# Causal attention on one core: the softmax's probabilities are turned block by block on VectorE and carried to their keys by transfers within SBUF, in place of transposes on TensorE

## The chip, the core and the metric

The kernel runs on one core of one Trainium2 chip. The time is the device time of one execution in microseconds (us). The core has TensorE (PE; its weight loads are listed apart as PEld), VectorE (DVE), ScalarE (ACT), GpSimd (POOL) and SyncE (SP), which here only issues transfers. Each engine works through its own list of instructions strictly in order. Transfers (DMAs) run on the 16 DMA engines that the profile counts.

## The reference, cut to what matters

The program is one decoder layer over x of shape (4, 512, 512): a gated delta-rule attention, a cross attention with quantized operands, then a block of causal grouped-query attention and a mixture of experts. The change is in the third part:

```python
q = rmsnorm(h @ wq, qnorm_w); k = rmsnorm(h @ wk, knorm_w); v = h @ wv   # 16 heads of 128, 4 key heads
q, k = rope(q), rope(k)
scores = einsum('bhqd,bhkd->bhqk', q, k) / sqrt(128)
scores = where(causal, scores, finfo.min)
attn = softmax(scores)
o = einsum('bhqk,bhkd->bhqd', attn, v)
x1 = x + o.reshape(B, S, H * DH) @ wo
```

For `o`, the sum runs over keys. TensorE sums over the partition axis, so the probabilities, which the softmax leaves with queries on partitions, have to be turned so that keys lie on partitions.

## The kernel before, in words

The tokens are 16 tiles of 128 (`i`, four tiles to a sequence; `c = i % 4`). A tile attends to the `c + 1` tiles of its sequence up to itself, so a row of probabilities has `nk = 128 * (c + 1)` entries. The 16 query heads are taken as 4 groups `g` of 4 heads `n` that share one key head.

- `scores(i, g)`, lines 1316 to 1345: for each head one f32 matmul of 128 queries by `nk` keys (L1333), the causal mask (L1335), the row maximum (L1336, L1337), the exponential on ACT (L1339), and the division by the row sum on DVE (L1341, L1343). The result is four tiles `e[n]` of queries x keys; even groups use the buffers `xa`, odd ones `og` and `x_in`, one set each.
- `values(g, e)`, lines 1354 to 1373: for each key tile `k`, four TensorE transposes (L1364), a copy of the four results from PSUM to SBUF on ACT (`eT`, L1366, three buffers), and one f32 matmul of 512 columns that adds to `po` (L1370, and L1360 for the last `k`). Then DVE copies `po` to `oT` (L1372).
- `project(g)`, lines 1375 to 1382: four f32 matmuls of 512 columns per group, `oT` times the output weights (L1380), with the weights' next pieces loaded by SP into three buffers (`wot`, `c_o`; `load_o`, L1239).
- `attention(i)` runs `scores(g + 1)`, `project(g - 1)`, `values(g)` for each g; the first group of the next tile is scored under the last group of this one.

Around it, `weave` (L155) mixes five streams into one program: attention of tile i, q/k/v projections of a later tile (`qkv`, weights through four `c_q` buffers, L1230 and L1267), the cross attention of a later tile (`crossing`, L283 to L371), the end of an earlier tile (`rest_of`, L1421) and the routing of tokens to experts. Each stream is a generator; `weave` advances the stream with the lowest due time, and `steps` (L152, L153) says how many pauses a stream is expected to have, so how much of a tile's time one pause stands for. ACT, DVE and POOL keep the order of this program; PE's and SP's lists are ordered by the scheduler that builds the program. At the end `load_experts` (L1690 to L1694) loads 12 MB of expert weights through SP while the last tiles are attended to, and the experts follow.

SP issues every one of these loads. A transfer counts into one of eight semaphores in turn, and an issue waits until the transfer eight before it has landed. So at most eight are on their way.

Of the kernel before, what the change touches and what calls it, by code (L numbers as in the profile page):

```python
# [31 lines left out]
F32 = mybir.dt.float32  # L32
BF16 = mybir.dt.bfloat16
AF = mybir.ActivationFunctionType
ALU = mybir.AluOpType
# [4 lines left out]
P = 128  # L40
B, S, D = 4, 512, 512
NT = B * S // P
TB = S // P
KD = D // P
# [60 lines left out]
def decoder(ctx: ExitStack, tc: tile.TileContext, a: dict, out: bass.AP):  # L105
    nc = tc.nc
# [6 lines left out]
    ident = tab[:, C_ID, :]  # L113
# [36 lines left out]
            yield from g  # L150

    steps = {"first_o": 3, "cross": 37, "qkv": 12, "rest_of": 5, "route": 10, "enter": 8, "spares": 24, "load": 26}  # L152
    steps.update((f"attention{c}", n) for c, n in enumerate((37, 41, 53, 57)))  # L153

    def weave(*streams):  # L155

# [53 lines left out]
    def transposed(src, pool, name, bufs=2):  # L210

        kind, eye = (F32, ident) if src.dtype == F32 else (BF16, ident_i)
        tp = p_b.tile([P, KD, P], kind, name="pb")
        for kd in range(KD):
            nc.tensor.transpose(tp[:, kd, :], src[:, kd * P : (kd + 1) * P], eye)
        t = pool.tile([P, KD, P], kind, name=name, bufs=bufs)
        nc.scalar.copy(t, tp)
        return t
# [23 lines left out]
    hTs, x2s, xis, fronts = {}, {}, {}, {}  # L242
# [135 lines left out]
    with ExitStack() as st:  # L378
# [18 lines left out]
        p_b = st.enter_context(tc.tile_pool(name="a_pb", bufs=4, space=PSUM))  # L397
# [675 lines left out]
        start = prologue(0)  # L1073
# [68 lines left out]
    with ExitStack() as st:  # L1142
        keep = st.enter_context(tc.tile_pool(name="b_keep", bufs=1, reuse_waits="tile"))
        small = st.enter_context(tc.tile_pool(name="b_small", bufs=4, reuse_waits="tile"))
        p_b = st.enter_context(tc.tile_pool(name="b_pb", bufs=6, space=PSUM, reuse_waits="tile"))
# [3 lines left out]
        wa = st.enter_context(tc.tile_pool(name="b_a", bufs=2, reuse_waits="tile"))  # L1149
        mid = st.enter_context(ExitStack())  # L1150
        wq_ = mid.enter_context(tc.tile_pool(name="b_q", bufs=2, reuse_waits="tile"))
# [39 lines left out]
        def norms(i):  # L1191


            x2 = x2s.pop(i)
            x3 = wq_.tile([P, D], F32, name="x3", bufs=1)
            yield from layernorm(x3.unsqueeze(1), x2.unsqueeze(1), small)
            nc.sync.dma_start(x3d[i], x3)
            h = wq_.tile([P, D], F32, name="h3", bufs=1)
            ss = small.tile([P, 1], F32, name="rms_s")
            nc.scalar.activation(h, x3, AF.Square, accum_out=ss)  # L1200
            yield
            r = small.tile([P, 1], F32, name="rms_r")
            rsqrt(r, ss, small, add=1e-6, mul=1.0 / D)
            yield
            nc.vector.tensor_scalar(h, x3, r, None, ALU.mult)
            yield
            tp = p_b.tile([P, KD, P], F32, name="pb")
            hTs[i] = wq_.tile([P, KD, P], F32, name="hT", bufs=2)
            for kd in range(KD):
                nc.tensor.transpose(tp[:, kd, :], h[:, kd * P : (kd + 1) * P], ident)  # L1210
            for kd in range(KD):
                nc.scalar.activation(hTs[i][:, kd, :], tp[:, kd, :], AF.Identity, scale=ln1[:, kd : kd + 1])
            yield
# [35 lines left out]
                load_o()  # L1249
                yield  # L1250

        zero = wa.tile([P, 4, P], F32, name="eT", bufs=3).rearrange("p a b -> p (a b)")
        nc.gpsimd.memset(zero, 0.0)
        nc.gpsimd.dma_start(hd[CAP : CAP + P], zero)
        nc.gpsimd.dma_start(spares[0 : 2 * NE * P].rearrange("(p n) c -> p (n c)", p=P), zero[:, 0 : 4 * NE])
# [60 lines left out]
        def scores(i, g, out):  # L1316

            c = i % TB
            at = (i - c) % RING
            runs = [(0, at, min(c + 1, RING - at))]  # L1320
            if at + c + 1 > RING:
                runs.append((RING - at, 0, at + c + 1 - RING))
            nk = (c + 1) * P
            qT, rq = qs[i]
            both = 2 if c < 2 else 1
            e = [ao.tile([P, S], F32, name="xa", bufs=4) for _ in range(4)] if g % 2 == 0 else [ao.tile([P, S], F32, name=n, bufs=2) for n in ("og", "og", "x_in", "x_in")]
            es = small.tile([P, 4], F32, name="es")
            nm = small.tile([P, 4], F32, name="nm")
            for n in range(0, 4, both):
                ps = p_b.tile([P, both, S // both], F32, name="pb")  # L1330
                for m in range(both):
                    for k, j, w in runs:
                        nc.tensor.matmul(ps[:, m, k * P : (k + w) * P], qT[g][:, n + m, :], kT[:, g, j : j + w, :], start=True, stop=True)  # L1333
                diag = ps[:, :, nk - P : nk]
                nc.vector.tensor_tensor(diag, diag, over(tab[:, C_CAUSAL, :], both), ALU.add)  # L1335
                nc.vector.tensor_reduce(nm[:, n : n + both], ps[:, :, :nk], AX.X, ALU.max, negate=True)  # L1336
                nc.vector.tensor_scalar(nm[:, n : n + both], nm[:, n : n + both], rq, None, ALU.mult)  # L1337
                for m in range(both):
                    nc.scalar.activation(e[n + m][:, :nk], ps[:, m, :nk], AF.Exp, bias=nm[:, n + m : n + m + 1], scale=rq, accum_out=es[:, n + m : n + m + 1])  # L1339
                yield  # L1340
            nc.vector.reciprocal(es, es)  # L1341
            for n in range(4):
                nc.vector.tensor_scalar(e[n][:, :nk], e[n][:, :nk], es[:, n : n + 1], None, ALU.mult)  # L1343
            out.append(e)
            yield

        def attention(i):


            c = i % TB  # L1350
            vals = [kv[k] for k in range(i - c, i + 1)]
            oTs = []

            def values(g, e):
                po = p_1.tile([P, 4, P], F32, name="po")
                eTs = []
                for k in range(c + 2):
                    if k > c:
                        yield
                        nc.tensor.matmul(po, vals[c][:, g, :], eTs[c], start=c == 0, stop=True)  # L1360
                        break
                    tp = p_b.tile([P, 4, P], F32, name="pb")
                    for n in range(4):
                        nc.tensor.transpose(tp[:, n, :], e[n][:, k * P : (k + 1) * P], ident)  # L1364
                    eT = wa.tile([P, 4, P], F32, name="eT", bufs=3)
                    nc.scalar.copy(eT, tp)  # L1366
                    eTs.append(eT)
                    yield
                    if k:
                        nc.tensor.matmul(po, vals[k - 1][:, g, :], eTs[k - 1], start=k == 1, stop=False)  # L1370
                oTs.append(wa.tile([P, 4, P], F32, name="oT"))
                nc.vector.tensor_copy(oTs[-1], po)  # L1372
                yield

            def project(g):
                oT = oTs.pop(0)
                for h in range(0, 4, 2):
                    w = ahead_o.pop(0)
                    for m in range(2):
                        nc.tensor.matmul(pw, oT[:, h + m, :], w[:, m, :], start=g == 0 and h + m == 0, stop=g == 3 and h + m == 3)  # L1380
                    load_o()
                    yield

            es = early.pop(i, [])
            if not es:
                yield from scores(i, 0, es)
            for g in range(4):
                if g < 3:
                    yield from scores(i, g + 1, es)
                elif i + 1 < NT:  # L1390
                    while i + 1 not in qs:
                        yield
                    early[i + 1] = []
                    yield from scores(i + 1, 0, early[i + 1])
                if g == 1:
                    pw = p_1.tile([P, D], F32, name="pw")
                if g > 0:
                    yield from project(g - 1)
                if g == 3:
                    x3 = wa.tile([P, D], F32, name="x3_in")  # L1400
                    nc.sync.dma_start(x3, x3d[i])
                yield from values(g, es.pop(0))
            del qs[i]
            yield
            yield from project(3)
            nc.vector.tensor_tensor(x3, pw, x3, ALU.add)
            xs[i] = x3
# [13 lines left out]
        def rest_of(i):  # L1421

            x1 = xs.pop(i)
            x2 = ao.tile([P, D], F32, name="acc", bufs=1)
            nc.sync.dma_start(x2, x2d[i])
            ss = small.tile([P, 1], F32, name="rms_s")
            h = wa.tile([P, D], F32, name="h2", bufs=1)
# [7 lines left out]
            nc.gpsimd.tensor_tensor(x2, x2, x1, ALU.add)  # L1435
            stored.append(nc.sync.dma_start(out[i * P : (i + 1) * P], x2).ins.name)
            yield
            hT = transposed(h, wa, "eT", bufs=3)
            yield

            parts = p_b.tile([P, P], F32, name="pb")
# [326 lines left out]
        def turned(b):  # L1768
            t = rows_of.pop(b)
            tp = p_b.tile([P, KD, P], F32, name="pb")  # L1770
            for kd in range(KD):
                nc.tensor.transpose(tp[:, kd, :], t[:, kd, :], ident)
            hTs[b] = wa.tile([P, KD, P], F32, name="eT", bufs=3)
            nc.vector.tensor_copy(hTs[b], tp)

        def gate_up(b):
# [128 lines left out]
```

## Time and profile before

| | |
|---|---|
| median of 3 runs | 3339.76 us (3336.23 to 3340.16) |
| profiled execution | 3333.82 us, of which the span from first to last instruction is 3332.0 us |
| mean granted TensorE clock | 0.984; 1.00 (0.99 in two stretches) in the stage that the change touches |
| the attention stage | from 1950 to 3095 us of the span |
| one tile of attention | the last add of a tile (L1406) ends at 2024.9, 2100.4, 2174.3, 2256.6, 2326.4 ... 2931.4 us: 906.5 us for 12 tiles, 75.5 us each |
| transfers that SP issues in a tile | about 30 |

"Busy" is the share of time in which an engine runs an instruction; matmuls are pipelined, so their listed durations overlap, and the cost of one is read from the distance between starts. An f32 matmul appears as two records. A group row gives count, busy time and mean duration, then the idle time of the engine just before and what ended it. The granted clock is the share of full TensorE speed.

### The profile page before, as it was taken

How to read it: one execution, taken by the hardware profiler on the slowest of the kernel's cores; microseconds unless marked ns; L12 is line 12 of the kernel's file. 1: busy time of each engine (PE TensorE's matmuls, PEld its weight loads, DVE VectorE, ACT ScalarE, POOL GpSimd, SP SyncE). 2: the span in 40 equal slices, each digit the busy share in tenths (PEclk: the TensorE clock that was granted, in tenths of full speed). 3: DMA queues.
4: the chain of work that ended last, by engine and by line, in shares of the span. 5: the costliest groups of instructions: out<-in, count | busy, mean ns of one | idle time of the engine just before them, and what ended most of it. 6: DMA issues, size and time to landing. Idle time of an engine off the chain costs nothing.

```text
span 3332.0 us, 48178 instructions
## 1 busy us (share of the span) xinstructions
PE 3170.1 (95%) x16015; PEld 1775.1 (53%) x16015; DVE 1829.9 (55%) x4184; ACT 1604.7 (48%) x4391; POOL 1460.5 (44%) x2780
## 2 busy tenths in 40 slices
PE   5899999999999999999998789999999999999998
PEld 3555555556555555555554445555555554555443
DVE  5755555546555556555454566556665666656211
ACT  3445555445554455545453345555555455644221
POOL 1156757676666766676764211112211221221442
PEclk8999999999999999999998899999999999999999
DMA  6343534444344434454434455546545555567443
GB/s 177 108 126 111 144 104 130 138 124 126 118 129 138 138 114 117 128 149 120 121 110 119 153 172 188 176 158 195 182 161 167 187 157 155 177 211 264 81 85 57
DMA packets 491033, 476.09 MB, mean 143 GB/s; under 512 B 225333, under 2 KB 340555, under 8 KB 490657
## 3 DMA queue, kind: packets, MB, share of 16 engines
q1 hardware_dynamic: 477616, 444.59, 44.3%
q0 software_dynamic: 11728, 25.58, 3.6%
q8 instruction: 128, 2.10, 0.3%
q10 hardware_dynamic: 1440, 2.84, 0.2%
q14 instruction: 121, 0.98, 0.1%
HBM read 411.23 MB, written 61.69 MB: 142 GB/s over the span
## 4 chain that ended last, share of the span: by engine, by line
PE 78%; DVE 10%; ACT 5%; issue 3%; DMA 3%; POOL 2%; SPq 0%; ACTq 0%; POOLq 0%; DVEq 0%
PE pb L598 25%; PE pb L1267 8%; PE pw L1380 5%; PE pb L972 5%; PE pb L1782 4%; DVE cv L609 3%; PE pb L1333 3%; PE po L1370 2%; PE pb L259 2%; PE pb L1364 2%; PE pb L686 2%; PE pb L671 2%; PE po L926 1%; PE po L1360 1%; PE ps L899 1%
## 5 line engine op out<-in xcount | busy, mean ns | idle before, releaser
L598 PE MATMUL pb<-xnT,w 128*128 128x512 f32 x2048 | 956.9, 602 | 0.5 <-DVE at L674 0.5
L598 PEld LDWEIGHTS pb<-xnT,w 128*128 128x128 f32 x2048 | 364.2, 192 | 337.0 <-issue 330.6
L609 DVE SCALAR_TENSOR_TENSOR cv<-pb,pp,cv 128x510 f32<-128x510 f32 (+2 forms) x576 | 424.3, 746 | 98.9 <-ACT cv L606 85.6
L752 POOL TENSOR_TENSOR iT<-iT,iW 64x126 f32<-64x126 f32 (+22 forms) x930 | 344.4, 370 | 72.9
L1267 PE MATMUL pb<-c_q,hT 128*128 128x512 f32 x768 | 352.4, 599 | 3.4 <-DMA c_q<-in_c_wq_dram 1.8
L751 POOL TENSOR_TENSOR iW<-iA,iT 64x126 f32<-64x126 f32 (+22 forms) x930 | 318.7, 343 | 65.7 <-issue 0.2
L1186 POOL TENSOR_TENSOR rope_s<-q,tab 128x128 f32<-128x128 f32 x80 | 44.9, 561 | 481.3 <-DVE q L1297 368.3
L972 PE MATMUL pb<-wot,og 128*128 128x512 f32 x512 | 246.5, 605 | 5.5 <-DVE xa L977 4.5
L1267 PEld LDWEIGHTS pb<-c_q,hT 128*128 128x128 f32 x768 | 141.4, 192 | 157.6 <-issue 146.1
L606 ACT ACTIVATE cv<-pb,pp 128x512 f32<-128x512 f32 x192 | 148.5, 774 | 146.7 <-PE pb L598 142.7
L653 POOL TENSOR_TENSOR rk<-ss,mhalf 128x8 f32<-128x8 f32 x32 | 77.9, 2436 | 277.2 <-DVE ss L652 277.2
L977 DVE TENSOR_TENSOR xa<-pb,xa 128x512 f32<-128x512 f32 x112 | 77.1, 688 | 186.9 <-PE pb L972 186.8
L306 ACT ACTIVATE x_e<-pb,nm,x_step 128x256 f32<-128x256 f32 x256 | 141.1, 565 | 58.3 <-DVE nm L302 53.6
L1333 PE MATMUL pb<-kT,qT 128*128 128x256 f32 (+3 forms) x576 | 163.2, 409 | 0.8 <-ACT og L1339 0.7
L1380 PE MATMUL pw<-wot,oT 128*128 128x512 f32 x344 | 162.5, 599 | 1.3 <-DVE oT L1372 1.3
L705 POOL TENSOR_TENSOR qg<-qh,row 128x512 f32<-128x512 f32 x64 | 83.2, 1300 | 178.5 <-ACT qh L612 155.6
L972 PEld LDWEIGHTS pb<-wot,og 128*128 128x128 f32 x512 | 92.6, 192 | 99.8 <-issue 88.0
L612 ACT ACTIVATE qh<-cv 128x512 f32<-128x512 f32 x64 | 40.4, 631 | 213.7 <-DVE cv L609 205.8
L1782 PE MATMUL pb<-w_gu,eT 128*128 x288 | 129.9, 594 | 2.8 <-issue 2.0
L1366 ACT COPY eT<-pb 128x512 f32<-128x512 f32 x160 | 91.5, 596 | 84.4 <-PE pb L1364 83.5
L458 ACT ACTIVATE em<-em,ee 128x128 f32<-128x128 f32 x256 | 78.3, 388 | 95.7 <-POOL ee L655 81.5
L1333 PEld LDWEIGHTS pb<-kT,qT 128*128 128x128 f32 x576 | 97.7, 191 | 48.6 <-issue 29.6
(436 smaller groups left out, 6171.1 us busy)
## 6 DMA issues: line engine op xcount, KB each, us to landing
c_q<-in_c_wq_dram SPq DMA_DIRECT2D x128, 512.0 KB
w<-in_a_w_dram SPq DMA_DIRECT2D x124, 512.0 KB
wot<-in_c_wo_dram SPq DMA_DIRECT2D x86, 512.0 KB
row<-g_d SPq DMA_DIRECT2D x64, 512.0 KB
c_o<-in_c_wo_dram SPq DMA_DIRECT2D x42, 512.0 KB
at_d<-at SPq DMA_DIRECT2D x64, 256.0 KB
T<-t_d SPq DMA_DIRECT2D x32, 512.0 KB
X<-x_d SPq DMA_DIRECT2D x32, 512.0 KB
```

Of the source, the lines that this page charges most:

```text
L306: nc.scalar.activation(e[:, 2 * r + g, :], ps[r][:, g, :], AF.Exp, bias=nm[:, r, g : g + 1], scale=step[:, h : h + 1], accum_out=ssum[:, g ...
L598: nc.tensor.matmul(pj, wt[:, kd, p * P : (p + 1) * P], xnT[:, kd, :], start=kd == 0, stop=kd == KD - 1)
L606: nc.scalar.activation(ac, pj, AF.Identity, bias=cb[:, m, h : h + 1], scale=cw[:, m, h, 3:4])
L609: nc.vector.scalar_tensor_tensor(ac[:, j:], pj[:, : S - j], cw[:, m, h, 3 - j : 4 - j], ac[:, j:], ALU.mult, ALU.add)
L751: eng.tensor_tensor(u, A[:, i, i + 1 :].unsqueeze(2).to_broadcast([nb, n, w]), T[:, i, :w].unsqueeze(1).to_broadcast([nb, n, w]), ALU.mult)
L752: eng.tensor_tensor(T[:, i + 1 :, :w], T[:, i + 1 :, :w], u, ALU.add)
L972: nc.tensor.matmul(pw, og[p][:, c * P : (c + 1) * P], wot[:, p, :], start=p == 0, stop=p == HG - 1)
L1267: nc.tensor.matmul(pj, hT[:, kd, :], w[:, kd % 2, :], start=kd == 0, stop=kd == KD - 1)
L1333: nc.tensor.matmul(ps[:, m, k * P : (k + w) * P], qT[g][:, n + m, :], kT[:, g, j : j + w, :], start=True, stop=True)
L1366: nc.scalar.copy(eT, tp)
L1380: nc.tensor.matmul(pw, oT[:, h + m, :], w[:, m, :], start=g == 0 and h + m == 0, stop=g == 3 and h + m == 3)
L1782: nc.tensor.matmul(pg, hT[:, kd, :], w_gu[:, bass.ds(e, 1), kd, :, :], start=kd == 0, stop=kd == KD - 1)
```

## The change

1. The transposes on TensorE and the copies to `eT` go. After the division, four VectorE instructions turn each head's probabilities in 32x32 blocks into one tile `t` (128 partitions x 4 nk, one buffer). A block transpose moves nothing out of its quarter of 32 partitions, so 16 transfers per group (four quarters q by four blocks b) bring each quarter's rows to the partitions of its keys. They are issued by SP, move 32 partitions of `nk` f32 each (16 to 64 KB), and land in the `e` tiles themselves, which now hold keys x (heads, 32 queries).
2. The value matmuls take the `e` tiles directly: 4 (c + 1) matmuls of 128 columns in place of (c + 1) of 512.
3. `po` is copied by ACT, not DVE, into its old order.
4. `steps` is set to the new numbers of pauses. Buffers are made to fit: `norms` normalizes into `x2` and `hT` and needs no `h3`; `x3_in` has one buffer, not two; `rest_of` and the experts use `hT` and `oT` where they used `eT`.

```diff
-    steps.update((f"attention{c}", n) for c, n in enumerate((37, 41, 53, 57)))
+    steps.update((f"attention{c}", n) for c, n in enumerate((79, 71, 77, 75)))
...
-            h = wq_.tile([P, D], F32, name="h3", bufs=1)
+            hTs[i] = wq_.tile([P, KD, P], F32, name="hT", bufs=2)
...
-            nc.scalar.activation(h, x3, AF.Square, accum_out=ss)
+            nc.scalar.activation(hTs[i].rearrange("p k t -> p (k t)"), x3, AF.Square, accum_out=ss)
...
-            nc.vector.tensor_scalar(h, x3, r, None, ALU.mult)
+            nc.vector.tensor_scalar(x2, x3, r, None, ALU.mult)
...
                 nc.vector.tensor_scalar(e[n][:, :nk], e[n][:, :nk], es[:, n : n + 1], None, ALU.mult)
+            yield
+
+            t = wa.tile([P, 4 * S], F32, name="eT", bufs=1)[:, : 4 * nk].rearrange("p (b k n i) -> p b k n i", b=4, n=4, i=32)
+            for n in range(4):
+                nc.vector.transpose(t[:, :, :, n, :].rearrange("p b k i -> p k b i"), e[n][:, :nk].rearrange("p (k b j) -> p k b j", b=4, j=32))
+                if n % 2:
+                    yield
+            for q in range(4):
+                for b in range(4):
+                    nc.sync.dma_start(e[q][b * 32 : (b + 1) * 32, :nk], t[q * 32 : (q + 1) * 32, b].rearrange("p k n i -> p (k n i)"))
+                yield
             out.append(e)
...
-                eTs = []
-                for k in range(c + 2):
-                    if k > c:
-                        yield
-                        nc.tensor.matmul(po, vals[c][:, g, :], eTs[c], start=c == 0, stop=True)
-                        break
-                    tp = p_b.tile([P, 4, P], F32, name="pb")
-                    for n in range(4):
-                        nc.tensor.transpose(tp[:, n, :], e[n][:, k * P : (k + 1) * P], ident)
-                    eT = wa.tile([P, 4, P], F32, name="eT", bufs=3)
-                    nc.scalar.copy(eT, tp)
-                    eTs.append(eT)
+                for q in range(4):
+                    for k, val in enumerate(vals):
+                        nc.tensor.matmul(po[:, q, :], val[:, g, :], e[q][:, k * P : (k + 1) * P], start=k == 0, stop=k == c)
                     yield
-                    if k:
-                        nc.tensor.matmul(po, vals[k - 1][:, g, :], eTs[k - 1], start=k == 1, stop=False)
                 oTs.append(wa.tile([P, 4, P], F32, name="oT"))
-                nc.vector.tensor_copy(oTs[-1], po)
+                nc.scalar.copy(oTs[-1].rearrange("p n (q i) -> p q n i", q=4), po.rearrange("p q (n i) -> p q n i", n=4))
                 yield
...
-                    x3 = wa.tile([P, D], F32, name="x3_in")
+                    x3 = wa.tile([P, D], F32, name="x3_in", bufs=1)
...
-            hT = transposed(h, wa, "eT", bufs=3)
+            hT = transposed(h, wa, "hT", bufs=1)
...
-            hTs[b] = wa.tile([P, KD, P], F32, name="eT", bufs=3)
+            hTs[b] = wa.tile([P, KD, P], F32, name=("oT", "oT", "hT")[b % 3], bufs=(2, 2, 1)[b % 3])
```

More of the change, by code (lines that the diff above doesn't have):

```diff
@@ L1204, in norms @@
             yield
-            nc.vector.tensor_scalar(h, x3, r, None, ALU.mult)
+            nc.vector.tensor_scalar(x2, x3, r, None, ALU.mult)
             yield
             tp = p_b.tile([P, KD, P], F32, name="pb")
-            hTs[i] = wq_.tile([P, KD, P], F32, name="hT", bufs=2)
             for kd in range(KD):
-                nc.tensor.transpose(tp[:, kd, :], h[:, kd * P : (kd + 1) * P], ident)
+                nc.tensor.transpose(tp[:, kd, :], x2[:, kd * P : (kd + 1) * P], ident)
             for kd in range(KD):
@@ L1250, in first_o @@
                 yield
-        zero = wa.tile([P, 4, P], F32, name="eT", bufs=3).rearrange("p a b -> p (a b)")
+        zero = wa.tile([P, 4 * S], F32, name="eT", bufs=1)[:, 0:S]
         nc.gpsimd.memset(zero, 0.0)
```

## The prediction

> **What bounds the kernel now.** I read the shares by stretch of time first, then the groups by line, then the order of time on PE, DVE and SP. By stretches (start:end, length, busy PE, PEld, DVE, ACT, POOL with counts, granted clock, DMA share, GB/s):
>
> ```profile
> 2326.00:2625.00 299.00, 294.28 (x1339) 167.61 (x1338) 187.54 (x533) 157.50 (x426) 64.87 (x92) 1.00 0.56 175
> 2625.00:2931.00 306.00, 295.99 (x1291) 157.16 (x1290) 189.84 (x546) 165.18 (x443) 68.74 (x94) 0.99 0.56 167
> 3025.00:3075.00 50.00, 49.91 (x173) 24.90 (x172) 31.78 (x97) 26.62 (x58) 5.97 (x6) 1.00 1.02 349
> 3075.00:3095.00 20.00, 20.00 (x84) 10.67 (x83) 5.98 (x21) 4.70 (x9) 5.96 (x7) 1.00 0.60 154
> ```
>
> PE is busy 97 to 100% of the attention stage, DVE 62%, ACT 53%, the DMA engines 56%; only from 3025 to 3075, while the expert weights load, are the DMA engines full too. PE's list is the bound, so PE work taken away is worth its full length as long as what feeds PE keeps up. The groups that the change removes or splits:
>
> ```profile
> L1370 PE MATMUL po<-eT,val 128*128 128x512 f32 x192 | 100.2, 607 | 1.0 <-ACT eT L1366 0.2
> L1366 ACT COPY eT<-pb 128x512 f32<-128x512 f32 x160 | 91.5, 596 | 84.4 <-PE pb L1364 83.5 <-ACT eT L1366 0.7
> L1360 PE MATMUL po<-eT,val 128*128 128x512 f32 x128 | 67.2, 607 | 0.3 <-ACT eT L1366 0.3
> L1372 DVE COPY oT<-po 128x512 f32<-128x512 f32 x64 | 43.9, 686 | 37.7 <-PE po L1360 34.7 <-issue 2.8
> ```
>
> Neither transposes nor values make PE wait long. Their true cost is the distance between starts in the order of time on PE:
>
> ```profile
> 2410.99 1.02 PE L1370 MATMUL po<-eT,val 128*128 128x512 f32 x2
> 2411.85 0.60 PE L1364 MATMUL pb<-tab,xa 128*128 128x128 f32 x4
> 2412.28 1.02 PE L1370 MATMUL po<-eT,val 128*128 128x512 f32 x2
> ```
>
> A 512-column f32 matmul (two records) takes 2411.85 - 2410.99 = 0.86 us, four transposes 0.43 us. For f32 matmuls of 128 columns with changing weights, the delta-rule stage has the row (also in order of time):
>
> ```profile
> 1000.46 0.61 PE L908 MATMUL ps<-r,X 128*128 128x128 f32 x4
> 1000.90 1.88 PE L598 MATMUL pb<-xnT,w 128*128 128x512 f32 x4
> ```
>
> Four records, two matmuls, in 0.44 us: 0.22 us each.
>
> **PE's list.** Over 16 tiles there are 4 x 40 = 160 (group, key tile) pairs. Removed: 160 x 4 transposes of 0.108 = 69 us. Values: before 160 x 0.86 = 138 us, after 640 x 0.22 = 141 us. Together **-66 us**. Separate waits come on top: in the built program the value matmuls have 503 instructions that only wait (a quarter's first matmul needs four transfers). Such an event instruction on PE's sequencer lasts 51 ns at L1364; 503 x 0.051 = 26 us if all of it shows, 0 if matmuls in flight cover it. I take half, **+13 us**, since a quarter's matmuls (0.22 to 0.88 us) are as short as two to four waits at c = 0 and longer later.
>
> **ACT and DVE.** ACT loses 160 copies (91.5 us) and gains 64 of nearly the same shape (64 x 0.596 = 38 us): no path, 0. DVE loses 43.9 us and gains 256 block transposes, 64 of each width. No row shows one. Below, the division's L1343 (0.24 us at 128, 0.48 at 512 elements); above, DVE reading PSUM (L1335 0.293 at 128, L1336 0.69 at 512); farthest, L1343's longest single record, 1.18 us. I take the PSUM row, 64 x (0.29 + 0.42 + 0.55 + 0.69) = 125 us, so DVE rises by 81 us over 1145 us, from 62 to 70%. It stays under PE; alone it costs 0, and its cover is that PE's queue is ahead of it.
>
> **SP and the transfers.** This is where I expect the price. New are 64 x 16 = 1024 issues where SP now makes about 30 per tile. The nearest rows, on SP in order of time:
>
> ```profile
> 1798.74 6.41 SPq L1103 DMA_DIRECT2D x_kT<-x_kT_d  x12
> ...
> 2431.16 0.34 SPq L271 DMA_DIRECT2D x_q_d<-x_qi  x1
> 2435.04 5.09 SPq L279 DMA_DIRECT2D x_qT<-x_q_d  x3
> ```
>
> One issue alone is 0.34 us, twelve of 32 partitions in a row 6.41 / 12 = 0.53 us. L279 must wait until L271's transfer has landed: 2435.04 - 2431.50 = 3.5 us, and 1.4 us at 1789.40, before the stage was loaded; the longest such wait is 4.6 us. I take 0.44 us an issue and 2.5 us to land: 16 x 0.44 = 7.0 us a group, 28 us a tile. The others take about 26 x 0.42 + 4 x 1.87 = 18 us a tile (L279 has four at 1.87). SP has 46 us of work in a tile of 75.5 us, so by sum it is no bound, but it works in order, and it now carries something that values wait for.
>
> The chain per group, from the last score matmul: softmax to the end of the division 6.5 us (2680.7 to 2687.2, and 2707.4 to 2714.0), block transposes 2.0 (mean of the four widths), issues 7.0, landing 2.5, so 18.0 us; plus what stands ahead in SP's queue, 0 to 8 us (the set of L279 takes 7.5), I take 4: **22 us**. Against it stands the lead: in the order in which the changed program is built, the PE work between a group's last score matmul and its first value matmul, counted with the rates above, is 22 us in the mean, but under 20 in 24 of 64 groups, under 18 in 11, and 13.6 at the least. So half of the groups would be late, by some 4 us: 32 x 4 = 128 us. A late group lets the next one's chain run on meanwhile (a group takes 75.5 / 4 = 19 us, the lead spans more than one), so I count half, **+64 us**. Bounds: at 0.34 an issue, landing 1.4 and an empty queue the chain is 15.3 us, about none late, 0; with 0.53, 4.6 us and 8 ahead it is 30 us, all 64 late by 8, half of which is 256 us.
>
> Rule against row: the Trainium skill, "DMA: Bandwidth & Descriptors", section "Bandwidth", says that transfers under 64 KB are dominated by their descriptors and should be gathered to a megabyte; these have 16 to 64 KB, which speaks against the change. Its fixed 2.0 us per transfer (section "Anatomy of one DMA", stated for GpSimd's path) would make the chain half a microsecond shorter, an estimate. No run here shows it for transfers within SBUF.
>
> **The end.** The last tiles have nothing beside them. In the built order SP issues 11 expert loads and about four other loads between the transfers of the last tile's first and second group. From 3025 to 3075 the queue moves 349 GB/s, so a 512 KB load takes 1.5 us and 15 take 22 us, where a group before took about 12 us: +10. Eight transfers in flight make the first ones after such a set land 8 x 1.5 us late, of which I count 7; the last group's chain (transposes 2.7, issues 7.0, landing 2.5 from the division's end at 3076, then 3.5 us of values) ends 3 us after the 3089.5 of now. Together **+20 us**, bounds 0 and 45.
>
> **The small edits cost 0.** `norms` writes into `x2`, which first must be stored by POOL's transfer; its six microseconds of normalization cover the 1.4 to 4.6 us that a landing takes, and 16 x 2 us off PE's path is the worst. One buffer for `x3_in`: the tile before is stored half a tile earlier. The sum of 0 stands within the other terms' width.
>
> **Sum**, in the profiled execution's own terms: 3333.8 - 66 + 13 + 64 + 20 = 3364.8. The median of the runs lies 5.9 us above that execution (3339.76 against 3333.82), so the forecast for the runs is **3371 us**, 0.9% slower. A measurement of this kernel can tell about 0.2% (7 us) from no change.
>
> **Rivals.**
> - *The lead covers the chain* (faster). For it: PE's lead grows with the pauses, 22 us in the mean; SP has 30 us free in a tile. Then lateness is 10 us, the end 10: 3333.8 - 66 + 13 + 10 + 10 = 3301, 3307 in the runs' terms. 0.33.
> - *The one tile `t` decides* (much slower, DVE and SP in turn). DVE may not turn group g + 1 before group g's 16 transfers have landed, and while DVE waits, all its other work waits. A round is transposes + issues + landing: 2.0 + 7.0 + 2.5 = 11.5 us, with L279's set inside one round of a tile some 57 us a tile, under PE's 71. With 2.7 + 8.5 + 4.6 and other loads inside (20 us) it is 83 us a tile; from 71 on it decides. 13 tiles x (83 - 75.5) = 98, with 30 at the end: 3462, 3468 in the runs' terms. 0.11.
> - *PE's list doesn't get shorter*: if 128-column passes went at the weight load's 0.190 us (LDWEIGHTS), 1280 x (0.19 - 0.11) = 102 us would eat the 66. The row at 1000.46 speaks against it. With lateness hidden by the longer list, 3333.8 - 66 + 13 + 102 + 20 = 3403, 3409. 0.04.
> - *They cancel*: lateness and end near 53 us together. 3340 give or take 7. 0.06.
>
> **How the numbers follow.** The forecast's case (3347 to 3440) has 0.46. Faster 0.33, same 0.06, slower 0.46 + 0.11 + 0.04 = 0.61. The forecast's own range is 3347 to 3440. The range for 8 in 10 reaches from 3290, below the faster case's centre, to 3455: out of it stay the lower third of the first rival (0.1) and the upper part of the second (0.07).
>
> **What would show it.** PE without transposes at L1364 and value matmuls 0.22 us apart; SP's list with 16 issues per group at 0.34 to 0.53 us; PE idle before the value matmuls put down to transfers, some 60 us in all; the tile period near 75.5 us still or above it. I am wrong if PE stays 97% busy and a tile takes 71 us (first rival), if the longest waits are DVE's transposes for transfers (second), or if value matmuls stand 0.38 us apart (third).

## The result, and the profile after

The changed kernel takes **3578.72 us** (median of 5 runs, 3575.10 to 3583.29) against 3340.16 for the kernel before (median of 5, 3336.23 to 3341.50): ratio 1.0713, 95% interval 1.0701 to 1.0725, slower by 238.6 us. The forecast was 3371 us: the sign was right, the loss over the kernel before was nearly eight times as large (238.6 us, not 31). The profiled execution took 3578.82 us.

First the engines' totals and the granted clock in 40 slices, from the page of the changed kernel:

```profile
span 3577.0 us, 51043 instructions
...
PE 3216.2 (90%) x16335; PEld 1845.4 (52%) x16335; DVE 1892.5 (53%) x4376; ACT 1555.2 (43%) x4295; POOL 1466.4 (41%) x2780
...
PEclk7999999999999999999988999989998999997999
```

Then the shares by stretch of time in the attention stage (start:end, length, busy PE, PEld, DVE, ACT, POOL with counts, granted clock, DMA share, GB/s). The first two stretches are those of the prediction:

```profile
2326.00:2625.00 299.00, 260.08 (x1225) 157.32 (x1224) 180.44 (x537) 130.50 (x361) 55.51 (x77) 0.92 0.59 177
2625.00:2931.00 306.00, 245.95 (x1068) 140.95 (x1067) 159.74 (x468) 116.64 (x329) 54.19 (x75) 0.89 0.55 166
3200.00:3330.00 130.00, 92.13 (x352) 55.24 (x351) 57.36 (x169) 31.03 (x70) 17.69 (x19) 0.81 0.73 222
```

PE was 97 to 98% busy at clock 0.99 to 1.00 and is 80 to 87% busy at 0.89 to 0.92. No engine is fuller than before and the DMA engines carry the same load: something makes PE wait. All of the loss lies in this stage. By the tiles' last adds, the first tile ends 30 us later than before, the next twelve take 1068.7 us instead of 906.5 (89 us a tile, not 75.5), the last three 214.8 instead of 162.7; from there to the end of the span both kernels take 237 us. 30 + 162 + 52 = 244 us.

Who waits for the transfers, from the waits of the stage (engine, tile and line, what it waited for: us in total, times, longest):

```profile
DVE eT L1347 <- DMA x_in<-eT: 98.5, 15, 14.6
...
PE po L1368 <- DMA og<-eT: 51.4, 14, 11.5
...
PE po L1368 <- DMA x_in<-eT: 34.0, 26, 2.7
...
DVE eT L1347 <- DMA xa<-eT: 29.7, 9, 10.8
```

PE's value matmuls wait for transfers, with those for `xa` some 107 us; and DVE stands 128 us before its block transposes, because the tile `t` is still being read. And SP's own waits before it issues a transfer:

```profile
SPq L1352 <- DMA c_q<-in_c_wq_dram: 64.3, 58, 2.7
SPq L1352 <- DVE eT L1347: 63.1, 24, 6.7
...
SPq L1352 <- DMA wot<-in_c_wo_dram: 14.9, 15, 2.8
```

The first and third rows are not data that the transfers need: they are the landing of a weight load eight transfers earlier, by the rule of eight on their way. With the rows of the other weights it is 101 us. The issues themselves, by line (count: duration in ns, least, median, longest), and as SP's list in order of time:

```profile
L1352 SPq DMA_DIRECT2D xa<-eT x512: 507/588/2756, 1962.9 to 3308.5; - x171
L1352 SPq DMA_DIRECT2D og<-eT x256: 507/586/2539, 1976.1 to 3320.6; - x128
```

```profile
2033.92 12.72 SPq L1352 DMA_DIRECT2D xa<-eT  x16
...
2056.62 2.41 SPq L1352 DMA_DIRECT2D og<-eT  x4
2059.07 1.10 SPq L1229 DMA_DIRECT2D c_q<-in_c_wk_dram  x2
2060.21 3.56 SPq L1352 DMA_DIRECT2D og<-eT  x4
2063.82 5.02 SPq L1352 DMA_DIRECT2D x_in<-eT  x8
```

One issue takes 0.59 us. A group's sixteen take 12.72 us in a row here, or 12.2 us with two loads among them (2056.62 to 2068.84); over all 64 groups, from the start of the first issue to the end of the last, the median is 12.4 us, the mean 13.5, the shortest 10.0 and the longest 23.1. The chain of waits, restricted to 1950 to 3350 us, begins like this, first in the kernel before and then in the changed one:

```profile
by line: PE pb L1267 18.4%; PE pw L1380 12.4%; PE pb L1782 8.5%; PE pb L1333 7.8%; PE po L1370 5.8%; issue 4.6%; PE pb L1364 3.7%; PE po L1360 3.4%; PE po L1798 2.5%; PE pb L259 2.5%; PE pw L1798 2.4%; PE pb L368 2.0%; PE pb L1275 1.6%; ACT
...
by line: SPq L1352 17.9%; PE pb L1266 11.7%; PE pw L1379 8.1%; issue 6.5%; DMA c_q<-in_c_wq_dram 5.4%; PE pb L1332 4.2%; SPq L279 3.1%; DMA xa<-eT 2.8%; PE po L1368 2.5%; DMA wot<-in_c_wo_dram 2.5%; DMA acc<-x2d 2.2%; DVE eT L1347 1.9%; DMA
```

In the kernel before, PE's projections headed this list and no SP line was near its head. Now SP's issuing of the transfers is its largest piece, 17.9% of 1400 us, some 250 us.

### The profile page after: what moved, and what is told of

Same layout as the page of the kernel before. It is cut to its first block, busy times and chain, and to the rows that moved or that the text cites. A ratio compares the mean times of both kernels' runs of the same rounds, so it can differ in the third digit from the quotient of the medians.

```text
span 3577.0 us, 51043 instructions
## 1 busy us (share of the span) xinstructions
PE 3216.2 (90%) x16335; PEld 1845.4 (52%) x16335; DVE 1892.5 (53%) x4376; ACT 1555.2 (43%) x4295; POOL 1466.4 (41%) x2780
## 4 chain that ended last, share of the span: by engine, by line
PE 61%; DMA 11%; DVE 10%; SPq 9%; ACT 4%; issue 4%; POOL 1%; ACTq 0%; DVEq 0%; POOLq 0%
PE pb L598 23%; SPq L1352 7%; PE pb L1266 5%; PE pb L972 5%; PE pb L1781 3%; PE pw L1379 3%; DVE cv L609 3%; DMA c_q<-in_c_wq_dram 2%; PE pb L1332 2%; PE pb L671 1%; PE pb L686 1%; PE po L926 1%; PE ps L899 1%; SPq L279 1%; PE ps L908 1%
## 5 line engine op out<-in xcount | busy, mean ns | idle before, releaser
L1266 PE MATMUL pb<-c_q,hT 128*128 128x512 f32 x768 | 368.9, 623 | 30.3 <-DMA c_q<-in_c_wq_dram 17.2
L1379 PE MATMUL pw<-wot,oT 128*128 128x512 f32 x344 | 185.6, 666 | 27.2 <-DMA wot<-in_c_wo_dram 16.1
L1295 ACT ACTIVATE q<-pb 128x512 f32<-128x512 f32 x64 | 38.2, 597 | 224.7 <-PE pb L1266 222.3
L132 POOL TENSOR_TENSOR rms_r<-rsq,mhalf 128x1 f32<-128x1 f32 x48 | 27.3, 570 | 247.8 <-DVE rsq L131 242.3
L1296 DVE TENSOR_TENSOR q<-pb,qw 128x512 f32<-128x512 f32 x64 | 43.9, 685 | 148.9 <-ACT q L1295 146.8
L1379 PEld LDWEIGHTS pw<-wot,oT 128*128 128x128 f32 x344 | 68.5, 213 | 103.8 <-issue 72.4
```

What stands on the lines that cost most here:

```text
L1266: nc.tensor.matmul(pj, hT[:, kd, :], w[:, kd % 2, :], start=kd == 0, stop=kd == KD - 1)
```

## The experiments

Theory A after this reading: **what costs is SP's time per issue**, sixteen in a row in each group, at 0.6 to 0.8 us instead of the 0.44 of the forecast. Rivals: B, the landing and the single tile `t`; C, the bytes or the DMA engines; D, the small edits; E, the weights that come late behind the issues. Ratios are against the kernel before in the same batch, whose medians lie between 3336.8 and 3342.0 us.

### Is it the transfers, and are bytes or issues the price?

**No transfers.** The sixteen issues are taken out, the pauses stay; the values are computed from probabilities that were not turned.

```diff
-                for b in range(4):
-                    nc.sync.dma_start(e[q][b * 32 : (b + 1) * 32, :nk], ...)
                 yield
```

> The changed kernel without its 1024 transfers; the block transposes on VectorE stay, but the value matmuls read the unturned probabilities, so the attention's result is not the reference's. Theory A (the transfers through SP's list are the whole price): the stage is bound by TensorE again and 66 us of its list are gone, so 3334 - 66 = 3268 us, at most 3290. Rival B (block transposes on VectorE and the copy of po on ScalarE, which are in this run too, are a good part of the price): above 3400 us.

3270.77 us, ratio 0.9794 (0.9775 to 0.9813): 69 us faster than before. PE is full again, at its old clock:

```profile
2326.00:2625.00 299.00, 290.95 (x1488) 179.97 (x1487) 211.16 (x614) 153.34 (x429) 69.72 (x97) 0.99 0.58 183
```

So PE's list is shorter by what was forecast, DVE's transposes, which this run keeps, cost nothing, and the transfers cost 308 us (3578.72 - 3270.77), more than the whole loss.

**Four transfers of 128 partitions** and **eight of 64**: the same bytes in fewer issues.

```diff
-                    nc.sync.dma_start(e[q][b * 32 : (b + 1) * 32, :nk], t[q * 32 : (q + 1) * 32, b]...)
+                nc.sync.dma_start(e[q][:, :nk], t[:, q]...)                                  # four
+                    nc.sync.dma_start(e[q][b * 32 : (b + 2) * 32, :nk], t[b * 32 : (b + 2) * 32, q]...)   # eight: b = 0, 2
```

> The same bytes in 4 transfers per group of 128 partitions each instead of 16 of 32 partitions; the rows land on the wrong keys, so the attention's result is not the reference's. Theory A1 (the number of issues on SP, 0.59 us each, is the price): 256 issues are left, some 770 x 0.6 = 460 us less on SP's list, and the time falls to 3280 to 3340 us. Rival C (the bytes within SBUF on the DMA engines, and the loads that they hold up, are the price): stays above 3500 us.

> Edit: eight transfers of 64 partitions in a group, the same bytes, to the wrong keys (source and target partitions are the same, so the probabilities do not reach their keys): all else as in the changed kernel. So far: no transfers 3271 us, four of 128 partitions 3312, sixteen of 32 partitions 3579. Theory of a lead that covers the chain up to a point (the turn decides only when 16 issues of 0.6 us make it longer than the group's lead): 3320 to 3370. Rival (each issue costs the same, wherever): 3271 + 8 x 19 = 3425, 3400 to 3450.

Four: 3311.72 us, 0.9918 (0.9900 to 0.9936), inside theory A's range. Eight: 3374.69 us, 1.0097 (1.0081 to 1.0112), just above the first range and below the second.

| issues per group, same bytes | 0 | 4 | 8 | 16 |
|---|---|---|---|---|
| us | 3271 | 3312 | 3375 | 3579 |
| us more per issue added to a group | | 10 | 16 | 26 |
| first to last issue of a group, median us | | 2.5 | 5.7 | 12.4 |

C falls: with the bytes unchanged the loss goes with the number of issues. It grows faster than their number, and there is no sharp threshold either: both pure forms expected for the run with eight were wrong. The time of one issue hardly depends on its size. In the kernel with four:

```profile
L1351 SPq DMA_DIRECT2D xa<-eT x128: 464/592/1504, 1962.1 to 3043.4; - x128
```

0.592 us for 128 partitions, 0.588 for 32.

**By HBM**, five issues a group and all of it computed: `t` goes out in one transfer and comes back in four, which there may gather from four blocks at once.

```diff
+            nc.sync.dma_start(d, t.rearrange("p b k n i -> p (b k n i)"))
...
+                nc.sync.dma_start(e[q][:, :nk], d[q * 32 : (q + 1) * 32].rearrange("j (b x) -> b j x", b=4))
```

> t goes to HBM in one transfer of 128 partitions, and four transfers of 128 partitions bring it back to its keys: 5 issues per group instead of 16, twice the bytes, two landings one after the other; everything is computed. Theory A1 (number of issues): 5 x 0.45 = 2.3 us of SP per group in place of 9.6, the second landing costs 2 to 4 us of a lead of 22: 3290 to 3360 us. Rival C (bytes): 84 MB in place of 42, above 3579.

3625.09 us, 1.0863 (1.0833 to 1.0893): far outside theory A's range, and where rival C had put it, which counted twice the bytes. Fewer than a third of the issues, and slower than the change. SP's longest wait in the stage shows another reason than the bytes:

```profile
SPq L1356 <- DMA turn_d<-eT: 331.2, 62, 11.5
```

The first transfer back must wait until `t` has landed in HBM, and SP, in order, stands still for it, 5.3 us each time. So it isn't the count of issues alone that matters, but SP's time, standing included. How much of this run's loss is that standing and how much the longer way and its bytes, the run with POOL further below tells in part.

### What does SP's time do: hold up the group, or the weights?

**The small edits alone**, in the kernel before (`norms` through `x2`, one `x3_in`, `rest_of`'s own `hT`):

> Edit: the kernel before with only the change's edits beside the turn: the norm in x2's place without tile h, x3_in in one buffer, the third stage's hT in its own tile. All theories: 3340 +- 10 us. If these edits have a part in the loss (x3_in in one buffer above all, whose load waits for the tile before), it is over 3355.

3343.42 us, 1.0002 (0.9993 to 1.0012). D falls.

**Issues that nobody waits for**, in the kernel before, TensorE turning as ever; sixteen transfers per group from a table into a spare tile.

```diff
+                for b in range(4):
+                    nc.sync.dma_start(spare[b * 32 : (b + 1) * 32, :nk], flat[q * 32 : (q + 1) * 32, :nk])
```

> Edit: the kernel before with the small edits, TensorE turning the probabilities as before, and beside it 16 transfers of 32 partitions from the table to a tile that nobody reads, issued in each group from SP where the change issues its own; nothing waits for them. It adds only SP's time and DMA traffic. Theory of the issue price by the loads (SP's queue is full, weights and x come late): +60 to +150 us, 3400 to 3490. Theory of the chain (turn, issue and landing in a row before the values are what costs; SP itself has room): within 20 us of the kernel before, 3325 to 3365.

3566.53 us, 1.0665 (1.0644 to 1.0686), outside both ranges. It measured more than was meant: the four quarters write the same places of `spare`, so each issue waits until the last writer has landed:

```profile
SPq L1348 <- DMA spare<-tab: 248.9, 118, 7.6
```

The second form writes 32x64 to a place of its own each time:

```diff
-                    nc.sync.dma_start(spare[b * 32 : (b + 1) * 32, :nk], flat[q * 32 : (q + 1) * 32, :nk])
+                    nc.sync.dma_start(spare[b * 32 : (b + 1) * 32, (g % 2 * 4 + q) * 64 : (g % 2 * 4 + q + 1) * 64], flat[q * 32 : (q + 1) * 32, :64])
```

> Edit: as the run with the issues alone, but the 16 extra transfers of a group carry 32x64 each to places that no other transfer of this group or the next writes, so that SP has only to issue them and waits for no landing (in the run with the issues alone SP waited 248.9 us for spare's earlier transfers). Theory that SP's time of issue alone is what costs (1024 x about 0.6 us = 600 us more on one queue in a stage of 1150 us, weights late behind it): 3460 to 3570 us. Rival, that it was SP's standing for landings: 3340 to 3400 us.

3409.62 us, 1.0222 (1.0205 to 1.0239), between the ranges and close to the lower one. So E, as far as issues alone bring it about, is worth about 73 us: SP's list is fuller by 606 us of issues and loads come late, while no other work waits for the transfers. PE's largest wait in the stage is then one for weights:

```profile
PE pb L1266 <- DMA c_q<-in_c_wq_dram: 19.3, 6, 7.0
```

A SyncE that besides issuing stands 249 us costs 157 us more (the first form also moved more bytes, which these two don't separate).

**Another queue for half of the issues, or all.** In `nc.sync.dma_start`, `nc.sync` becomes `(nc.gpsimd if b % 2 else nc.sync)`, or `nc.scalar` for those, or `nc.gpsimd` for all sixteen.

> Edit: of the 16 transfers of a group the eight with odd b are issued by POOL and not by SP. Theory of the issue price (SP's 16 issues of about 0.6 us in a row are the larger part of a group's turn, and DVE's next block transposes wait for their end): SP's part falls from about 10 to about 5 us in a group, so some 5 us x 60 groups is the most that can come back; with the part of it that is on the chain, 3430 to 3520 us. Rival (the landing and the single buffer t, whoever issues): within 30 us of the changed kernel, 3550 to 3600. Rival (POOL's own price for an issue, with its work of 41% of the span in between): slower than 3590, and the waits of L1347 for x_in and xa grow.

> Edit: the eight transfers with odd b are issued by ScalarE's queue. Theory of the issue price: SP's part halves as with POOL, but each issue on ACT stands in ACT's own order, behind exps and copies that wait for PE, so less comes back: 3450 to 3560 us. Rival (an issue on ACT costs ACT what it costs SP, 0.6 us x 8 in 60 groups = 290 us of an engine that is busy 43%, and the evictions of PE's banks come late by it): slower than 3580. Rival (landing and t alone): within 30 us of 3579.

> Edit: all 16 transfers of a group are issued by POOL. Theory of SP's time (weights and rows late behind the issues on SP): SP is as free as before the change, what is left is the group's chain with POOL's 16 x 0.5 = 8 us of issue and DVE's wait for t: 3380 to 3460 us. Rival (the chain of 16 issues in a row, on whichever engine, sets the pace): 3500 to 3590 us. Rival (POOL's rope of q comes late behind 16 issues): over 3460, and DVE's wait for rope_s grows over 66 us.

Half on POOL: 3421.58 us, 1.0245 (1.0218 to 1.0273), 157 us under the changed kernel, a little more than theory A expected. The DMA engines move the same bytes, only the issuing is spread. Half on ACT: 3540.68, 1.0590 (1.0572 to 1.0607), inside theory A's range: an issue costs ACT 0.60 us, and among those who wait for it are ACT's own squares, exponentials and evictions:

```profile
  ACT q L1295: 92.8, 14
  ACT x_e L306: 80.4, 9
  ACT q L1168: 67.4, 6
  ACT oT L1371: 64.7, 7
```

All on POOL: 3489.82, 1.0469 (1.0451 to 1.0487), as the third expectation had it. SP is as free as before the change, and yet it is 68 us worse than half and half: sixteen issues at 0.50 us are again in one row, and the rotation of q stands behind them (66 us in the run with half):

```profile
DVE q L1189 <- POOL rope_s L1187: 119.6, 56, 7.9
```

So the row of issues in each group is a cost on any engine. That late weights are the smaller part of the loss is likely but not shown: in the run with free issues SP never waits for a group's probabilities, while in the changed kernel it stands 63 us before the transfers for DVE's transposes alone, and the loads behind stand with it.

The Trainium skill, "DMA: Bandwidth & Descriptors", section "Issuing engines are not separate DMA queues", says that initiating on several engines saves only the sequencer's time, "which is usually small relative to the DMA itself". The first half agrees with these runs. For one transfer the second half agrees too: an issue of 0.59 us is small beside the 5.3 us for which SP stood for a landing in HBM. But sixteen in a row make 16 x 0.59 = 9.4 us per group, and here the sequencer's time was not small: spreading half of the issues took 157 us off.

**By HBM, with the way back issued by POOL** (`nc.sync` becomes `nc.gpsimd` in the four transfers back):

> Edit: the way by HBM again (one transfer of t out by SP, four back), but the four that come back are issued by POOL, so that POOL and not SP stands until the first has landed (SP stood 331.2 us for it). Theory of SP's time: SP has one issue more in a group than the kernel before: 3300 to 3400 us. Rival (the way's own length, 5 us out and some us back, before the values): 3450 to 3620 us, with PE's and DVE's waits for these transfers as large as in the changed kernel.

3500.04 us, 1.0493 (1.0474 to 1.0511). SP is nearly as free as before the change (its issues take 265 us from 1980 to 2940, 249 before the change), 125 us come back with the same bytes, and the time lies in the rival's range: the way itself is long, and PE waits for it. What of the rest is the bytes, these runs don't separate.

```profile
PE po L1373 <- DMA xa<-turn_d: 37.8, 16, 13.2
PE po L1373 <- DMA og<-turn_d: 34.9, 8, 9.9
```

### The single tile t

**Two tiles `t`** (`bufs=2`); the room comes from leaving out q's norm weights.

> The changed kernel with two tiles t instead of one; to make room, the norm weights of q are left out (k's 512 are used for all groups of q and k), which changes values but no instruction's shape. Theory A2 (the single tile t makes VectorE wait for the transfers of the group before, 128 us, and with it everything on its list): 3579 falls by 100 us or more, to below 3480. Theory A1 (SP's list of 1024 issues in order is the bound whatever the buffer): stays within 40 us of 3579.

3521.46 us, 1.0537 (1.0518 to 1.0556): 57 us better, between the two expectations. DVE no longer waits for `t`, PE's values still wait 89 us for transfers. B is a part, 57 of 239 us.

**Half on POOL and `t` in two halves**, so that the next group may begin after eight transfers:

> Edit: half of the transfers on POOL, as before, and t is two tiles of two blocks of keys each, so that DVE's next block transposes into the first half wait for the first eight transfers alone. It computes all of it. Theory of two parts (SP's time, and the wait for t that two tiles brought 57 us): 3360 to 3405 us, 20 to 60 below the run with half on POOL. Rival (with POOL's half the wait for t is gone already, 9.2 us in that run): within 15 us of 3422. Eight DVE operations for four on a path that is not DVE's: at most +10 us.

3412.10 us, 1.0236 (1.0218 to 1.0254), 9.5 us under the run with half on POOL: inside the rival's 15 us. Where the row of issues is short, `t` isn't what is late.

### Fewer groups the new way

Only the odd groups are turned the new way, the even ones by TensorE; in the first three runs they share the two halves of `t` as buffers, with the issues on SP, on SP and POOL, and all on POOL.

> Edit: two of the four groups of a tile (g odd) are turned the new way, the other two by TensorE as before the change; t in two halves, whose tiles the other groups use for their turned probabilities. All of it is computed. Theory of SP's time (the issues are half, SP is some 60% full in the stage, and a group's transfers have the time of two): half of TensorE's gain comes, 33 us, and 0 to 40 us are lost: 3307 to 3350. Rival (each group that is turned the new way costs its own 240/64 us): 3440 to 3480.

> Edit: as the run with every other group, and half of its transfers issued by POOL. Theory of SP's time: SP has 4 issues per group more than before, the chain of a group is 5 us shorter: 3300 to 3335 us, faster than the kernel before. Rival (what is left in the run with half on POOL, 150 us over the run without transfers, is not SP's): half of it stays, 3345 to 3390.

> Edit: as the run with every other group, and all of its transfers issued by POOL, SP as free as before the change. If SP's time is what is left of the loss in the two runs beside it: under both, 3295 to 3330. If POOL's 16 issues in a row before the rope of q cost as they did with all groups (DVE's wait for rope_s 119.6 us): 3340 to 3400.

3466.13 us (1.0376, 1.0362 to 1.0391), 3491.65 (1.0462, 1.0447 to 1.0478) and 3492.89 (1.0457, 1.0442 to 1.0471). The first lies where its rival was, the other two over both of their ranges. Spreading the issues made nothing better, so the loss here is another one. The profile of the first names it: ACT's eviction of TensorE's transposes now waits for transfers that still read the shared buffer, and ACT is in order too.

```profile
ACT eT L1391 <- DMA x_in<-eT: 45.0, 13, 7.4
```

With those for `og` it is 72 us in this kernel and 108 in the one with everything on POOL (the 94 us in the next expectation added a row of each). With tiles of their own (the room from q's norm weights in BF16):

```diff
-                    eT = two[:, k % 2]                    # halves of the tile t
+                    eT = wa.tile([P, 4, P], F32, name="eT2", bufs=2)
```

> Edit: every other group (g odd) turned the new way, all issues on SP, with t in one tile of its own and the other groups' probabilities in two tiles of their own, so that ACT's evictions no longer wait for transfers that read t (94 us of such waits in the run with every other group and shared tiles); the room comes from q's norm weights in BF16, rounded. Theory that the shared tiles spoiled that run and the loss goes with SP's share of time: 3310 to 3370 us. Rival (each group turned the new way costs its own share, the tiles were not it): 3440 to 3480.

> Edit: the same with half of the transfers issued by POOL. Theory of SP's time: 10 to 40 us under the run beside it, 3290 to 3345, the best chance of a version under both kernels. Rival (POOL's order with the rope of q costs as much as SP's time gives): within 15 us of the run beside it.

All on SP: 3405.53 us, 1.0196 (1.0182 to 1.0210). Half on POOL: 3360.46, 1.0060 (1.0046 to 1.0074). The first lies between its two expectations: half of the issues cost about a third. TensorE's half of the gain would give some 3306, so 100 us are lost with 8 issues per group in the mean, 308 with 16. The second came 45 us under the run beside it, a little more than the 10 to 40 expected, but stayed above its range of 3290 to 3345. It is the fastest version with transfers that computes the reference's result, 0.6% over the kernel before: spread over two queues and over twice the time, the transfers cost some 55 us, and TensorE gives back 33. Only runs that leave out part of the work, with no transfers or with four to the wrong keys, were faster than the kernel before.

Theory A holds, in a wider form than at first: the price is the time that an in-order queue spends on a group's transfers, standing included. It reaches PE in three ways: through the values of the group itself (107 us of waits), through the tile `t` (57 us by the run with two), and through the loads behind (73 us by the run with free issues).

## Why the prediction was wrong in size

- **PE's list, -66 us: right.** Without transfers the kernel is 69 us faster than the kernel before. The value matmuls stand 0.22 us apart: in PE's order of time eight records, four matmuls, follow each other in 2119.67 - 2118.78 = 0.89 us.

```profile
2118.78 1.05 PE L1368 MATMUL po<-og,val 128*128 128x128 f32 x8
2119.67 1.06 PE L1368 MATMUL po<-x_in,val 128*128 128x128 f32 x8
```

- **Waiting instructions on PE, +13 us: not separated.** They are there (503, 51 ns in the median), but the longest is 10.6 us: the waits for transfers sit in them.
- **DVE and ACT, 0: right.** The block transposes take about the PSUM row's times that were chosen: medians of 0.27, 0.40, 0.54 and 0.67 us at 128, 256, 384 and 512 columns, against 0.29, 0.42, 0.55 and 0.69.
- **SP's price, 0.44 us an issue, 7.0 us a group: the step that failed.** It measured 0.59 us for one and 12.4 us for sixteen, above the upper bound of 0.53 an issue too. Two things were missed. The rows taken were loads and a set of twelve; the profile before had a nearer row, 64 transfers within SBUF by the delta-rule stage:

```profile
L724 SPq DMA_DIRECT2D rq<-sr x64: 527/558/735, 78.1 to 1749.4; - x64
```

  That gives 16 x 0.56 = 9 us; the shortest of the 64 groups takes 10.0. Most of the rest is the rule of eight on their way: it stands in the description of the kernel, but no term priced it. Sixteen transfers in a row meet weight loads of 512 KB among the eight before them, and SP stands for their landing, 101 us in the stage by the trace. No run changed the limit itself.
- **Lateness, +64 us: wrong through the step before.** With 12.4 in place of 7.0 the chain is 27 us, not 22, against a lead of 22: by the prediction's own rule 64 x 5.4 / 2 = 173 us, an estimate; with the mean of 13.5 it is 208. The bounds, 0 to 256, held such values; the range didn't reach them, since it was built on the chosen price. In place of 64, these would have made the forecast 3480 or 3515 us. The halving in that rule was never tested. PE's waits for the transfers before the value matmuls came to 107 us, where the prediction looked for some 60.
- **The end, +20 us: too low.** The last three tiles lost 52 us, over the bound of 45, and the first tile 30 us, for which there was no term. (By its own numbers the last group's chain ends at 3091.7, 2 us after 3089.5 and not 3; this changes nothing.)
- **The small edits, 0: right** (1.0002).
- **Terms that were missing.** Loads that come late behind the transfers had none: 73 us where the issues stand alone. Nor had the granted clock, below.
- **The rival of the single tile `t`** was priced at 3468 us and given 0.11. Its 57 us a tile were 53.5 by its own terms (4 x 11.5 + 7.5). With the measured row a round is 2.0 + 12.4 + 2.5 = 16.9 us, four of them and L279's set 75 us a tile, over the 71 from which it decides. By the prediction's own sign, DVE's transposes waiting longest for transfers (128 us, against PE's 107), this rival would have won; the run with two tiles shows that it is a part only, 57 us.
- **The skill's rule that small transfers should be gathered** was named and given no price. The row of 0, 4, 8 and 16 issues shows it to hold here, though through SP's time and not through the DMA engines, whose share is about the same with sixteen issues as before (0.59 against 0.56) and was higher, 0.68 from 1980 to 2940 us, in the faster run with four.

What stays open: how the 308 us split. 73 for late loads and 57 for `t` come from runs of their own; the rest, put down to values that wait, was not isolated, and the waits may hide one another.

The granted TensorE clock is part of the loss. As a mean from 1980 to 2940 us it goes down with PE's busy share:

| | before | none | four | eight | half on POOL | two `t` | changed | by HBM |
|---|---|---|---|---|---|---|---|---|
| PE busy | 0.98 | 0.98 | 0.96 | 0.93 | 0.91 | 0.87 | 0.85 | 0.84 |
| granted clock | 1.00 | 1.00 | 0.99 | 0.97 | 0.96 | 0.94 | 0.92 | 0.91 |

The mean hides two levels. Stretch by stretch the trace of the changed kernel has the clock at 1.00 or at 0.50, and at 0.50 the same two records of a value matmul take 0.77 us in place of 0.38:

```profile
2362.10:2368.90 6.80, 3.27 (x37) 1.97 (x35) 4.39 (x21) 4.44 (x11) 0.00 (x0) 1.00 0.25 47
2368.90:2382.50 13.60, 6.27 (x12) 3.52 (x13) 2.52 (x7) 0.81 (x3) 0.00 (x0) 0.50 0.43 140
...
2348.16 0.38 PE L1368 MATMUL po<-xa,val 128*128 128x128 f32 x2
...
2369.25 0.77 PE L1368 MATMUL po<-og,val 128*128 128x128 f32 x2 [3.88 <-DMA og<-eT]
```

So PE's waits are paid again in what PE does after them. From 1950 to 3340 us the changed kernel has 255 us at half clock, the kernel before 3.4 us in its stage. PE is busy for 184 of the 255 us; at full clock that work would take 92. So at most some 92 of the 239 us are clock, an estimate; no run held the clock while PE waited. The Trainium skill, "TensorE: Matmul & The Clock Gate", section "HAM oscillation — how this bites in real kernels", says that idle gaps over some 3.4 us bring the clock down. This trace agrees in part: of the 20 stretches at half clock from 1980 to 2940 us, 8 begin during or just after a gap of PE over 3.4 us, and 12 at shorter gaps, of 1.4 to 3.3 us.

## What to carry to other kernels

Count issues, not bytes: take the price of an issue from a row of the same kind of transfer, take it for the whole burst with the waits that the limit of transfers on their way brings, and set that sum, not one issue, against the lead of the work that needs the data. Where an in-order queue that used to carry only early loads gets something urgent, price both directions: the urgent transfers behind the loads, and the loads behind them. A shared queue, a shared buffer or a second engine each move the wait; a short run without the suspected work at all (here 3271 us) tells first how much there is to find.

## What the runs showed of the hardware

- An issue of a transfer within SBUF took SP 0.59 us whether it covered 32, 64 or 128 partitions (medians 588, 592 and 592 ns), ACT 0.60 us, and POOL 0.50 us.
- With 1024 such issues in place (16 per group, 8 KB each) and nothing waiting for them, a kernel changed otherwise only by the small edits became 2.2% slower: SP's issues took 715 of 960 us then.
- Moving half of the issues to POOL took 157 us off with the same bytes on the same DMA engines.
- The granted TensorE clock stood at 1.00 or 0.50. Its mean from 1980 to 2940 us was 1.00 with PE 98% busy and 0.92 with PE 85% busy; 12 of the 20 stretches at 0.50 came at idle gaps of PE of only 1.4 to 3.3 us, the other 8 at longer ones.
